# Last cross attention: scores computed a second time in transposed form, sums of weights by columns of ones, no transposes of weights

## The chip, the cores and the metric

The kernel runs on one core of one Trainium2 chip. A core has a matrix engine (TensorE, in the profile PE for its matrix instructions and PEld for the loading of their stationary operand), a vector engine (VectorE, DVE), an activation engine (ScalarE, ACT), a general engine (GpSimd, POOL) and a queue engine (SyncE, SP) that issues transfers. The engines run side by side, each through its own list of instructions in order, and wait for each other by semaphores. The metric is the time of one execution on the device in microseconds (us). Durations inside an execution are read from one profiled execution.

## The reference

Four transformer blocks are applied in turn to `x` (8 sequences of 112 rows, 256 wide). All read one context, `ctx_768` (8 x 375 rows, 192 wide), and everything is fp32. Blocks L0 to L2 have heads of 64; the change touches the last block, L3, with 16 heads of 16. Its middle part is the last cross attention, cut here to what is computed:

```
h = layernorm(x, ln2_w, ln2_b)
q = (h   @ q_w + q_b).reshape(B, T, 16, 16)      # B=8, T=112
k = (enc @ k_w + k_b).reshape(B, S, 16, 16)      # S=375
v = (enc @ v_w + v_b).reshape(B, S, 16, 16)
attn = einsum('bhtd,bhsd->bhts', q, k) * 16**-0.5
attn = where(enc_mask[:, None, None, :], -inf, attn)
attn = softmax(attn, axis=-1)
ca   = einsum('bhts,bhsd->bthd', attn, v)
x    = x + ca.reshape(B, T, 256) @ out_w + out_b
```

Ahead of it stands a masked self attention of the same block (heads of 16, T x T scores), behind it a feed-forward part: `x + gelu(layernorm(x) @ mlp1_w + b) @ mlp2_w + b`, 256 to 1024 to 256.

## The kernel before

**Stages and steps.** The work is numbered in stages: 0 to 2 are block L0 (self attention, cross attention, feed-forward), 3 to 5 block L1, 6 the one attention of L2, 7 the masked self attention of L3, 8 the last cross attention, 9 the last feed-forward. An attention stage is a run of steps. Stage 8 has 32 steps: 8 sequences, and for each four groups g of four heads, the heads 8(g//2) + 2r + g%2 for r = 0..3. The four heads of a step lie on four different groups of 32 rows of the matrix engine. Two heads (of even and odd number) share such a group of 32 rows, 16 rows each; the key tile holds both, and there are two query tiles, one for each parity e, with zeros in the rows of the other parity, so that a product 32 rows deep gives the scores of one head.

**One step of stage 8.** `emit_s` writes the scores of the four heads, 112 queries by 375 keys each, into two PSUM tiles of two banks (four matmuls, L1078). The pool `ps_s` of these tiles has just two, so the next step's scores wait for both to be read. `softmax` (its branch for heads of 16) has VectorE add the mask, negate, and take the minimum, in one custom instruction for each head (L1011), with the result in SBUF; ScalarE takes the exponential of each head and accumulates its sum into a column of `bsums` (L1019). `emit_t` turns the weights, which stand as queries by keys, into keys by queries: for each of three chunks of keys (128, 128, 119) four transposes on TensorE (L1108) into one PSUM bank, and a copy to SBUF by ScalarE (chunks 0 and 2, L1118) or VectorE (chunk 1, L1115). `emit_pv` multiplies with the values (12 matmuls, L1141), which stand 32 columns a head with zeros in 16 of them, so that a pair of steps (both parities) accumulates into one PSUM tile; the second step of the pair copies it to `oT` (L1154).

**Once for each sequence** `emit_norm` takes the reciprocal of the 16 sums of each query (L1182), GpSimd spreads it to 256 columns (`rb`, L1183), and `emit_scale` transposes that in two pieces (L1189) and multiplies `oT` by it (L1198). Then the output product runs for a group of 128 rows of `x` (two chunks, L680) and VectorE adds it to `x` (L684).

**Filling jobs.** Keys of stage 8 come from a key job for each sequence (two products into two PSUM banks, L832 and L841, and two evacuations with the bias, L350 or L358). Values come from value jobs, two chunks of keys at a time (L907, L916), spread over the value tile by `spread_values` (GpSimd zeroes, L811, and VectorE adds the bias, L812). There are such jobs for normalisation, for its transposes, for queries, and for the feed-forward behind.

**What sets the order.** A planner in Python, `Plan`, writes the order of TensorE's work: every piece is an item with a cost in us, a due time, what it uses and makes, and what it has to come after. The main items of a step are S (scores), E (the second half of the exponentials), T (transposes, one item a chunk) and PV. The main loop (from L1610) goes through the steps; in each it emits the scores of a step ahead, the PV of two finished steps together, the T items of the next step with `plan.fill` after each, and then the rest of the filling jobs by the pace of the whole. The steps of stage 7 for late sequences are woven into the first half of stage 8. The other engines take their work in the order that the scheduler gives. Queries, keys and values live in one SBUF ring (`arena`, 10700 columns).

**Loads that the change touches.** `add_last_square` loads the three square weights of L3 into one tile (three transfers, L530); `add_masks` loads both masks to all rows (L560, L561) and multiplies the context mask out to `cm` by eight GpSimd instructions (L590); `bias_columns` (L415) turns small rows into columns of scales and biases.

Of the kernel before, what the change touches and what calls it, by code (L numbers as in the profile page):

```python
# [21 lines left out]
P = 128  # L22
# [9 lines left out]
EPS = 1e-5  # L32

# [271 lines left out]
def kernel(ctx: ExitStack, tc: tile.TileContext, a: dict, out: bass.AP):  # L305
# [3 lines left out]
    ARENA = 10700  # L309
# [16 lines left out]
    plan = Plan(RINGS, ARENA, lambda k: 512 if k[0] == "v" or k[0] == "q" and k[1] in TURNED else S if k[0] == "k" and k[1] in (1, 4, 6, 8) else 4 * T)  # L326
# [3 lines left out]
    def place(key):  # L330

        lo, hi = plan.place[key]
        t = arena[:, lo:hi]
        return t.rearrange("p (i t) -> p i t", i=2) if key[0] == "q" or hi - lo == 4 * T else t
# [7 lines left out]
    def evac(dst, src, n, scale=None, bias=None):  # L342
# [4 lines left out]
        if la <= ld:  # L347
# [58 lines left out]

    brows = const.tile([8, P], F32, name="brows")
    erows = const.tile([1, 2, P], F32, name="erows")
# [3 lines left out]
    bcols = const.tile([P, 10], F32, name="bcols")  # L412
    qcols = const.tile([P, 2, 4], F32, name="qcols")

    def bias_columns():  # L415
        ps = mm_tile()
        nc.tensor.transpose(ps[:, :8], brows, ident[:8, :8])
        for e in range(2):
            nc.tensor.transpose(ps[:, 8 + e : 9 + e], erows[:, e, :], ident[:1, :1])
        nc.vector.tensor_copy(bcols, ps[:, :10])  # L420
        for e in range(2):
            nc.vector.tensor_scalar_mul(qcols[:, e, :], bcols[:, 0:4], bcols[:, 8 + e : 9 + e])

# [8 lines left out]
    ctxB = const.tile([2 * KB, B * S], F32, name="ctxB")  # L432
# [91 lines left out]
    def add_last_square(key, names):  # L524


        def fn():
            t = wpool.tile([P, len(names), 2, D], F32, tag="w", name="squares")
            for i, (k, name) in enumerate(names):
                nc.sync.dma_start(t[:, i, :, :], a[name].rearrange("(c p) n -> p c n", p=P))  # L530
                got[k] = t[:, i, :, :]
# [21 lines left out]
    def add_masks():  # L553
# [4 lines left out]
        def load():  # L558
            m8 = wpool.tile([P, B * (T + S)], U8, tag="w", name="m8")
            nc.sync.dma_start(m8[:, : B * T], a["mask_BxS_bf0"].rearrange("b t -> (b t)").partition_broadcast(P))  # L560
            nc.sync.dma_start(m8[:, B * T :], a["mask_BxS2_bf0"].rearrange("b s -> (b s)").partition_broadcast(P))  # L561
# [20 lines left out]
        def place():  # L582
            got[key] = wpool.tile([T, B, S], BF16, tag="w", name="cm")

        plan.add_load(Item(("load", key), 0, place, makes=[key]))
        for b in range(B):

            def ctx_mask(b=b):
                c = B * T + b * S
                nc.gpsimd.tensor_scalar_mul(got[key][:, b, :], got[src][:T, c : c + S], NEG)  # L590

            plan.add(Item(("mask", b), 0, ctx_mask, first_of(7, 0) - 6 + 0.5 * b, uses=[src, key], seg=SEG[6]))

# [214 lines left out]
    def spread_values(t, ps, rows, bias):  # L808


        nc.gpsimd.memset(t.rearrange("p (g f) -> p g f", f=64)[:rows, :, 16:48], 0.0)  # L811
# [8 lines left out]
    def add_key_jobs(st, b, w, deadline, last=False):  # L820
# [4 lines left out]
        for u in range(1 if last else 4):  # L825
            keys = [("k", st, b, 2 * u + i) for i in range(2)]
            cell = []

            def begin(u=u, cell=cell):
# [8 lines left out]
            def fn(u=u, keys=keys, cell=cell):  # L838
                for i in range(2):
# [4 lines left out]
                    )  # L844
                for i in range(2):
                    t = place(keys[i])
                    evac(t, cell[i][:, :S], S, None, bcols[:, 6 + i : 7 + i] if last else None)
                    got[keys[i]] = t

            plan.add(Item(("kj", st, b, u), 2.1, fn, deadline(b, u), uses=[w], makes=keys, deps=ctx_deps(b),  # L850
                          seg=SEG[st], begin=begin))
# [39 lines left out]
    def add_last_values(st, w, deadline):  # L891
# [4 lines left out]
        for pair in pairs:  # L896
# [3 lines left out]
            def lhs(t, r, b, c):  # L900
                k0, kl = KCH[c]
                return t[r, b * S + k0 : b * S + k0 + kl]

            def begin(pair=pair, cell=cell):
                for b, c in pair:
                    ps = mm_tile()
                    nc.tensor.matmul(  # L907
                        ps[: KCH[c][1], :D], lhsT=lhs(ctxA, slice(0, KA), b, c), rhs=got[wv][:, 0:D],
# [4 lines left out]
            def fn(pair=pair, keys=keys, cell=cell):  # L913
                for n, (b, c) in enumerate(pair):
                    r = slice(n * KB, (n + 1) * KB)
                    nc.tensor.matmul(  # L916
                        cell[n][: KCH[c][1], :D], lhsT=lhs(ctxB, r, b, c), rhs=got[wv][r, D:],
                        start=False, stop=True,
                    )
                for n, (b, c) in enumerate(pair):  # L920
                    t = place(keys[n])
                    spread_values(t, cell[n], KCH[c][1], got[("ctx", "row")])
# [26 lines left out]
    steps = []  # L949
# [289 lines left out]

    def cross_step(st, dh, b, g, turn=False):  # L1240
        at[(st, b, g)] = len(steps)
        j, tb = b // 2, (b % 2) * T
        if dh == 64:
# [446 lines left out]
```

## Time and profile before

| | before |
|---|---|
| time, median of three runs | 1608.58 us (1606.09 to 1613.75) |
| the profiled execution | 1611.6 us, span of its instructions 1609.8 us |
| mean granted clock of TensorE in it | 0.981 |
| TensorE busy | 1534.6 us, 95% of the span |
| weight load busy | 1035.7 us, 64% |
| VectorE busy | 866.6 us, 54% |
| ScalarE busy | 724.5 us, 45% |
| GpSimd busy | 553.9 us, 34% |
| first scores of stage 8 | at 1376.4 us of the span |
| last output product of stage 8 | at 1577.4 us |

Busy time counts an engine's own work, not waiting, and engines overlap. The granted clock is the share of full speed at which TensorE is let run. In a line of instructions the tile written stands before the arrow and those read behind it, with their shapes; `x4` is the number of instructions. A matmul in fp32 shows as two matrix instructions, a transpose as one. In a line of a group the figures are the count, the busy time, the mean of one in ns, and the idle time of the engine just ahead of them with what ended it. `L1078` is line 1078 of the kernel.

### The profile page before, as it was taken

What the parts mean: (1) busy time and instruction counts of PE and PEld (TensorE: products, weight loads), DVE (VectorE), ACT (ScalarE), POOL (GpSimd) and SP (SyncE); (2) the same over time, 40 slices, a digit from 0 to 9 for tenths busy, and PEclk for the clock granted to TensorE, in tenths of its full rate; (3) what the DMA queues carried; (4) which work ended last, traced back from release to release, by engine and by line L of the source; (5) the groups of instructions that cost most, each with busy time, mean ns of one, the idle gap of its engine ahead of it and who ended that gap; (6) DMA issues with size and microseconds to landing.
All of it is one profiled execution on the core that took longest, in us unless ns stands there. A gap on an engine that the chain in (4) does not pass through costs nothing.

```text
span 1609.8 us, 28327 instructions
## 1 busy us (share of the span) xinstructions
PE 1534.6 (95%) x10452; PEld 1035.7 (64%) x10452; DVE 866.6 (54%) x1994; ACT 724.5 (45%) x2364; POOL 553.9 (34%) x801
## 2 busy tenths in 40 slices
PE   9998999999899989999999899899999997999999
PEld 8776666565558877665665566565566555666667
DVE  3664565565422265655656532355566674677662
ACT  3452444444321444444444331244455554687672
POOL 1334343444402234443434321443433346222110
PEclk9999999999999999999999999998999997999999
DMA  5175477667401046457576611045567677200000
GB/s 179 38 210 152 135 218 223 172 191 209 137 30 53 23 134 205 147 176 220 161 202 195 190 50 39 0 115 180 164 193 228 179 222 211 68 2 2 2 1 23
DMA packets 128305, 212.49 MB, mean 132 GB/s; under 512 B 11287, under 2 KB 112295, under 8 KB 128167
## 3 DMA queue, kind: packets, MB, share of 16 engines
q1 hardware_dynamic: 127927, 210.52, 44.6%
q8 instruction: 82, 1.34, 0.3%
q14 instruction: 56, 0.46, 0.1%
q10 hardware_dynamic: 240, 0.17, 0.0%
HBM read 122.45 MB, written 87.43 MB: 130 GB/s over the span
## 4 chain that ended last, share of the span: by engine, by line
PE 78%; DVE 6%; ACT 5%; issue 4%; DMA 4%; POOL 2%; SPq 0%; DVEq 0%; ACTq 0%; POOLq 0%
PE mm L680 12%; PE mm L714 10%; PE mm L1141 10%; PE s L1078 9%; PE mm L866 7%; PE mm L832 7%; PE mm L875 4%; PE mm L841 4%; PE mm L1387 3%; PE mm L791 3%; DMA stage<-b 3%; PE mm L1108 3%; ACT pr L1035 2%; DVE stage L1056 2%; PE mm L1422 2%
## 5 line engine op out<-in xcount | busy, mean ns | idle before, releaser
L1042 POOL TENSOR_TENSOR pr<-pr,rinv 128x750 f32<-128x750 f32 (+3 forms) x224 | 327.4, 1474 | 324.0 <-DVE rinv L1040 323.4
L1035 ACT ACTIVATE pr<-s,nm 128x375 f32<-128x375 f32 (+3 forms) x640 | 302.1, 492 | 252.3 <-DVE nm L1029 204.7
L1078 PE MATMUL s<-arena 64*128 64x375 f32 (+6 forms) x1792 | 223.7, 406 | 18.9 <-ACT pr L1035 13.6
L1056 DVE STREAM_TRANSPOSE stage<-pr 128x768 f32<-128x768 f32 (+2 forms) x218 | 206.5, 969 | 50.3 <-POOL pr L1042 41.3
L1029 DVE TENSOR_REDUCE nm<-s 128x2 f32<-128x750 f32 (+3 forms) x224 | 205.8, 950 | 36.5 <-PE s L1078 35.0
L354 ACT COPY arena<-mm 128x375 f32<-128x375 f32 (+4 forms) x197 | 100.6, 516 | 276.8 <-PE mm L875 125.1
L1141 PE MATMUL mm<-stage,arena 128*64 128x112 f32 (+5 forms) x3840 | 190.1, 269 | 18.0 <-DMA stage<-b 12.6
L1141 PEld LDWEIGHTS mm<-stage,arena 128*64 128x64 f32 (+5 forms) x3840 | 168.9, 134 | 59.5 <-issue 21.3
L1078 PEld LDWEIGHTS s<-arena 64*128 64x128 f32 (+3 forms) x1792 | 122.1, 183 | 108.1 <-issue 33.0
L362 DVE COPY arena<-mm 128x375 f32<-128x375 f32 (+5 forms) x175 | 102.4, 596 | 152.9 <-PE mm L875 82.5
L1019 ACT ACTIVATE pr<-pr,nm 112x375 f32<-112x375 f32 (+2 forms) x256 | 124.5, 491 | 29.5 <-DVE nm L1011 27.9
L1035 ACT ACTIVATION_READ_ACCUMULATOR pr<-s,nm 128x1 f32 (+1 forms) x640 | 135.1, 211 | 0.0
L610 POOL TENSOR_TENSOR rs<-ve,mhalf 128x1 f32<-128x1 f32 x70 | 39.6, 566 | 248.2 <-DVE ve L608 246.4
L1040 DVE RECIPROCAL rinv<-sums 128x2 f32<-128x2 f32 (+3 forms) x224 | 37.8, 169 | 135.8 <-ACT pr L1035 134.7
L866 PE MATMUL mm<-L_xattn_Wv,ctxA 128*128 128x512 f32 (+1 forms) x192 | 93.7, 611 | 2.6 <-ACT arena L352 1.3
L832 PE MATMUL mm<-ctxA,L_xattn_Wk 128*128 128x375 f32 x256 | 93.3, 490 | 2.3 <-ACT hT L350 1.3
L1001 POOL MEMSET pr<- 128x9 f32 (+1 forms) x218 | 22.6, 107 | 210.2 <-DVE stage L1056 192.3
L714 PE MATMUL mm<-hT,L_xattn_Wq 128*128 128x224 f32 x384 | 82.4, 361 | 3.5 <-DVE arena L362 1.5
L684 DVE TENSOR_TENSOR x<-mm,x 128x256 f32<-128x256 f32 x70 | 29.4, 420 | 101.9 <-PE mm L680 101.9
L1108 PEld LDWEIGHTS mm<-ident,pr 112*128 112x128 f32 (+2 forms) x600 | 66.8, 153 | 22.9 <-issue 9.3
L1108 PE MATMUL mm<-ident,pr 112*128 112x112 f32 (+2 forms) x600 | 77.3, 268 | 4.1 <-ACT pr L1019 3.2
L680 PE MATMUL mm<-L_xattn_Wo,oT 128*128 128x256 f32 x336 | 79.1, 390 | 0.8 <-ACT oT L354 0.8
(136 smaller groups left out, 2258.3 us busy)
## 6 DMA issues: line engine op xcount, KB each, us to landing
b<-stage SPq DMA_DIRECT2D x344, 192.0 KB, 3.6
stage<-b SPq DMA_DIRECT2D x86, 768.0 KB, 5.8
b<-stage SPq DMA_DIRECT2D x144, 128.0 KB, 3.8
stage<-b SPq DMA_DIRECT2D x36, 512.0 KB, 4.6
L_xattn_Wo<-in_L_xattn_Wo_dram SPq DMA_DIRECT2D x3, 1024.0 KB, 14.9
L_xattn_w_ff<-in_L_xattn_w_ff_dram SPq DMA_DIRECT2D x3, 1024.0 KB, 8.5
L_xattn_Wv<-in_L_xattn_Wv_dram SPq DMA_DIRECT2D x4, 512.0 KB, 6.8
L_xattn_Wq<-in_L_xattn_Wq_dram SPq DMA_DIRECT2D x2, 1024.0 KB, 6.0
```

Of the source, the lines that this page charges most:

```text
L680: nc.tensor.matmul(ps[:, :D], lhsT=oT[:, c, t * P : (t + 1) * P], rhs=got[wv or w][:, c, :], start=(c == 0), stop=(c == n - 1),)
L714: nc.tensor.matmul(ps[:, i * 2 * T : (i + 1) * 2 * T], lhsT=got[w][:, k, m * P : (m + 1) * P], rhs=hT[:, k, lo:hi], start=(k == 0), stop=( ...
L832: nc.tensor.matmul(ps[:, :S], lhsT=got[wv][:, (2 * u + i) * P : (2 * u + i + 1) * P], rhs=ctxA[:, cols], start=True, stop=False,)
L866: nc.tensor.matmul(ps[: KCH[c][1], :], lhsT=lhs(ctxA, slice(0, KA), c), rhs=got[w][:, hf * 512 : (hf + 1) * 512], start=True, stop=False,)
L1019: return nc.scalar.activation(pr, pr, AF.Exp, bias=nm, scale=-1.0, accum_out=bsums[(st, b)][:, h : h + 1])
L1029: nc.vector.tensor_reduce(nm[:, :, :ns], sv, AX.X, ALU.max, negate=True)
L1035: nc.scalar.activation(pr[:, bk, sl, :], sv[:, bk, sl, :], AF.Exp, bias=nm[:, bk, sl : sl + 1], accum_out=sums[:, bk, sl : sl + 1],)
L1042: nc.gpsimd.tensor_tensor(pr, pr, rinv[:, :, :ns].unsqueeze(3).to_broadcast([rows, 2, ns, nk]), ALU.mult)
L1056: nc.vector.transpose(dst, src)
L1078: nc.tensor.matmul(tiles[i][:, n % 2, (n // 2) * nk : (n // 2 + 1) * nk], lhsT=qap(h), rhs=kap(h), start=True, stop=True,)
L1108: nc.tensor.transpose(pt[:kl, m * T : (m + 1) * T], cell[h][:, c * P : c * P + kl], ident[:T, :T])
L1141: nc.tensor.matmul(po[p0 : p0 + dp, blk * T : (blk + 1) * T], lhsT=got[vk][:kl, hv * dp : (hv + 1) * dp], rhs=wt, start=(c == 0 and par(h) ...
```

## The change

In stage 8 the weights are not transposed any more. The step's scores are computed as before and used for one thing only, their maximum over the keys (two `tensor_reduce` of VectorE over two heads each, negated). The maxima of four heads are columns 16(1-e) + 32r of a tile of zeros; TensorE transposes it, and VectorE adds it (after a minimum that bounds it) into the query tile, into a row that is unused for this parity. The keys are therefore kept twice, one tile for each parity, each with zeros in the other head's rows but for a row of ones, against the maximum, and a row with the mask, against a row of ones in the queries. So a second set of 12 matmuls gives the scores with keys on the rows, masked and less the maximum, into the same two PSUM tiles; two exponentials of ScalarE write the weights (125 rows by 672), and the 12 products with the values read them. Keys are cut 125, 125, 125. A value tile has ones in the 16 columns a head where zeros were; the sums of the weights come out in 16 rows of the result, and for each sequence one matmul with a selecting tile spreads them, VectorE takes the reciprocal of 128 x 448 in PSUM and multiplies. The result then has 512 rows instead of 256, so the output weight is padded with zero rows and the product takes four chunks. The key job makes four evacuations and has four transfers copy the mask row from DRAM; the mask is multiplied out once (8 x 375). The main loop orders these steps so: scores of step n+1, transposed maxima of step n (T 0), the jobs in between, transposed scores of step n (T 1).

```diff
-    ARENA = 10700
+    ARENA = 10550
...
-            t = wpool.tile([P, len(names), 2, D], F32, tag="w", name="squares")
-            for i, (k, name) in enumerate(names):
-                nc.sync.dma_start(t[:, i, :, :], a[name].rearrange("(c p) n -> p c n", p=P))
-                got[k] = t[:, i, :, :]
+            t = wpool.tile([P, 2 * len(names) + 2, D], F32, tag="w", name="squares")
+            for i, (k, name) in enumerate(names[:-1]):
+                got[k] = t[:, 2 * i : 2 * i + 2, :]
+                nc.sync.dma_start(got[k], a[name].rearrange("(c p) n -> p c n", p=P))
+            k, name = names[-1]
+            got[k] = t[:, 2 * len(names) - 2 :, :]
+            nc.gpsimd.memset(got[k], 0.0)
+            w = a[name].rearrange("(m r e d) n -> m r d e n", r=4, e=2, d=16)
+            for m in range(2):
+                for r in range(4):
+                    nc.sync.dma_start(got[k][32 * r : 32 * r + 16, 2 * m : 2 * m + 2, :], w[m, r])
...
-        for b in range(B):
-            def ctx_mask(b=b):
-                c = B * T + b * S
-                nc.gpsimd.tensor_scalar_mul(got[key][:, b, :], got[src][:T, c : c + S], NEG)
+        def ctx_mask():
+            nc.gpsimd.tensor_scalar_mul(got[key], got[src][:B, B * T :], NEG)
+            got["masks"] = bounce.tile([B, S], F32, tag="masks", name="masks")
+            nc.sync.dma_start(got["masks"], got[key])
...
+            def spread(cell=cell, keys=keys):
+                for e in range(2):
+                    t = place(keys[e])
+                    for i in range(2):
+                        evac(t[:, i, :], cell[i][:, :S], S, pcols[:, e : e + 1], kcols[:, e, i : i + 1], i == 0)
+                    at = AUG(e) + 1
+                    rows = t.rearrange("(g f) i k -> f g i k", f=32)[at]
+                    for i in range(2):
+                        nc.sync.dma_start(rows[:, i, :], got["masks"][b : b + 1, :].to_broadcast([4, S]))
...
+        def emit_s():
+            tiles = [ps_s.tile([T, 2, 512], F32, tag="s", name="s") for _ in range(2)]
+            for r in range(4):
+                nc.tensor.matmul(
+                    tiles[r // 2][:, r % 2, :S], lhsT=got[qk][rows(r), m, cols], rhs=got[kk][rows(r), m, :],
+                    start=True, stop=True,
+                )
+            for i in range(2):
+                nc.vector.tensor_reduce(top[:, 2 * i : 2 * i + 2], tiles[i][:, :, :S], AX.X, ALU.max, negate=True)
...
+        def emit_max():
+            pt = mm_tile()
+            nc.tensor.transpose(pt[:, :T], nm, ident[:T, :T])
+            q = got[qk][:, m, cols]
+            nc.vector.scalar_tensor_tensor(q, pt[:, :T], -0.01 * NEG, q, ALU.min, ALU.add)
...
+        def emit_w():
+            tiles = [ps_s.tile([CH, 2, 512], F32, tag="s", name="s") for _ in range(2)]
+            for c in range(3):
+                for r in range(4):
+                    nc.tensor.matmul(
+                        tiles[r // 2][:, r % 2, c * T : (c + 1) * T],
+                        lhsT=got[kk][rows(r), m, c * CH : (c + 1) * CH], rhs=got[qk][rows(r), m, cols],
+                        start=True, stop=True,
+                    )
+            for i in range(2):
+                if e:
+                    w = ppool.tile([CH, 6 * T], F32, tag="pr", name="wt")
+                else:
+                    w = stage[:CH, 768 * (g + i) : 768 * (g + i) + 6 * T]
+                wt.append(w.rearrange("p (r x) -> p r x", r=2))
+                nc.scalar.activation(wt[i], tiles[i][:, :, : 3 * T], AF.Exp)
...
+        def emit_pv():
+            po = pairs.pop((st, b, m)) if e else mm_tile()
+            for c in range(3):
+                for r in range(4):
+                    h = 8 * m + 2 * r + e
+                    nc.tensor.matmul(
+                        po[rows(r), e * T : (e + 1) * T], lhsT=got[("v", st, b, 0, c)][:CH, 32 * h : 32 * h + 32],
+                        rhs=wt[r // 2][:, r % 2, c * T : (c + 1) * T], start=(c == 0), stop=(c == 2),
+                    )
...
+            def emit_scale():
+                dst = oT[:, 0:4, b * T : (b + 1) * T]
+                ps = mm_tile()
+                nc.tensor.matmul(ps[:, : 4 * T], lhsT=sel, rhs=dst, start=True, stop=True)
+                nc.vector.reciprocal(ps[:, : 4 * T], ps[:, : 4 * T])
+                nc.vector.tensor_tensor(dst, dst, ps[:, : 4 * T].rearrange("p (c t) -> p c t", t=T), ALU.mult)
...
-    add_products(8, 9, w("sq"), 2, after_norm(8), norm_by(9), ("sq", "oc"))
+    add_products(8, 9, w("sq"), 4, after_norm(8), norm_by(9), ("sq", "oc"))
...
+            if i + 1 in lasts:
+                plan.main(("T", i + 1, 1))
+                left -= plan.fill(min(left, 0.8))
...
+            if nxt < hi and nxt in lasts and nxt <= i + 3 and clear(nxt):
+                left -= plan.fill(0.4 * left)
+                plan.main(("S", nxt))
+                nxt += 1
...
+            if i + 2 in lasts and plan.items[("S", i + 2)].done:
+                left -= plan.fill(0.5 * left)
+                plan.main(("T", i + 2, 0))
```

## The prediction

> **What bounds the kernel now.** I read the busy table of the page first, then busy time in stretches of 40 us through the last cross attention, then the instructions of TensorE there in order of time, and last the groups of instructions by shape in the last 400 us.
>
> ```profile
> PE 1534.6 (95%) x10452; PEld 1035.7 (64%) x10452; DVE 866.6 (54%) x1994; ACT 724.5 (45%) x2364; POOL 553.9 (34%) x801
> ```
>
> TensorE is busy 95% of the span, so an edit counts by what it does to TensorE's work or to its idle time. In the stretches (columns: length, then busy time of TensorE, weight load, VectorE, ScalarE, GpSimd, then granted clock and DMA) the stage of the change shows the same, at 37.4 to 38.4 us of 40:
>
> ```profile
> 1400.00:1440.00 40.00, 37.36 (x466) 26.57 (x465) 31.54 (x143) 34.10 (x127) 6.20 (x15) 1.00 0.01 2
> 1440.00:1480.00 40.00, 38.39 (x434) 26.68 (x437) 30.19 (x105) 30.00 (x87) 9.99 (x17) 1.00 0.01 2
> 1480.00:1520.00 40.00, 37.36 (x401) 26.27 (x397) 28.25 (x117) 29.75 (x101) 9.20 (x14) 0.91 0.01 2
> ```
>
> From 1400 to 1560 TensorE idles 7 us, with 2.7 more from 1382: about 10. VectorE and ScalarE have a quarter free, and relieving them alone gives nothing. The order of TensorE's work (start, length, line, operands, matrix instructions; a matmul is two, a transpose one):
>
> ```profile
> 1421.39 1.46 PE L832 MATMUL mm<-ctxA,ctx_w 128*128 128x375 f32 x4
> 1422.78 0.90 PE L841 MATMUL mm<-ctxB,ctx_w 64*128 64x375 f32 x4
> 1423.61 0.66 PE L1078 MATMUL s<-arena 32*112 32x112 f32 x16
> 1424.20 1.40 PE L1108 MATMUL mm<-ident,pr 112*128 112x112 f32 x12
> 1425.53 1.12 PE L1078 MATMUL s<-arena 32*112 32x112 f32 x16
> 1426.58 1.36 PE L1141 MATMUL mm<-stage,arena 128*32 128x112 f32 x48
> 1427.87 1.11 PE L1108 MATMUL mm<-ident,pr 112*112 112x112 f32 x8
> 1428.82 1.04 PE L907 MATMUL mm<-ctx_w,ctxA 128*128 128x256 f32 x4
> 1429.79 0.70 PE L916 MATMUL mm<-ctx_w,ctxB 64*128 64x256 f32 x4
> 1430.42 0.90 PE L1078 MATMUL s<-arena 32*112 32x375 f32 x8
> 1431.25 0.41 PE L1189 MATMUL mm<-ident,rb 112*128 112x112 f32 x2
> ```
>
> Start to start this prices: 12 weight transposes 1.33, a key job 2.22 (L832, L841), 8 narrow score matmuls .59, the weighted sums of two steps 1.29 (L1141), a value job 1.60 (L907, L916), the scores of a step .83, the two transposes of the sums .25. A score tile is handed on and used at once, since between scores and sums lie other steps' transposes. The groups by shape, last 400 us (count, then busy, mean ns, idle before):
>
> ```profile
> L1019 ACT ACTIVATE pr<-pr,nm 112x375 f32<-112x375 f32 x128 | 76.7, 604 | 21.5 <-DVE nm L1011 21.3
> L1011 DVE CUSTOM_DVE_ANT_0 pr<-s,cm 112x375 f32<-112x375 f32 x128 | 62.6, 544 | 4.3 <-PE s L1078 3.9
> L1108 PE MATMUL mm<-ident,pr 112*128 112x112 f32 x256 | 35.4, 269 | 3.5 <-ACT pr L1019 3.2
> L1029 DVE TENSOR_REDUCE nm<-s 128x2 f32<-128x750 f32 x28 | 25.0, 930 | 1.6 <-PE s L1078 1.4
> L1182 DVE RECIPROCAL rsum<-bsums 112x16 f32<-112x16 f32 x11 | 2.7, 249 | 5.9 <-ACT pr L1019 5.9
> ```
>
> **TensorE's work.** Gone: 32 sets of 12 transposes by 1.28 (they stand 1.24 to 1.33 apart) = 41.0, and eight pairs of sum transposes by .25 = 2.0. Added: 32 sets of 12 transposed score matmuls, 32 rows deep and 112 wide, which the 8 narrow scores price at .59 x 12/8 = .88, so 28.2 (from below the 12 sums matmuls of a step, .65, so 20.8); 32 transposes of the maxima by .13 = 4.2; eight column-sum matmuls 448 wide by .5 (estimate from the 375-wide key matmuls of L841, .42 each) = 4.0; output products of four chunks in place of two, seven token groups by .97 (1.13 as listed, .97 to the next start) = 6.8. Together 43.2 for 43.0, **+0.2 us**, between -7 (by the bound from below) and +13 (a set at the 1.28 of the twelve transposes it replaces); the narrow scores are the nearest row, the same operation with the same depth.
>
> **The new chain.** Scores and transposed scores share the same two PSUM tiles, and each uses both. So from the end of one set of transposed scores to the end of the next: first exponential .85 (125x672; the gate activation of the feed-forward, 128x384 in .58 and 128x512 in .69, has a slope of .86 ns a column), scores .75, the two maxima 2 x .93, the addition into q .30, the handovers .2, the transposed scores .9: **4.85 us a step** of which TensorE works 1.65. The rest has two gaps: .97 before the scores (the exponential holds the tile) and 2.17 before the transposed scores (VectorE's maxima and addition). A gap is idle unless TensorE has other work queued in exactly that place. Its order in the changed kernel says what stands there, priced with the rows above:
> - Second gap: in ten steps nothing but the maxima's transpose (.13) or that and a sums pair: 20 us idle. Two with little work: 2.6. Seven with a value job: .44 each, 3.1. The steps with a key job (2.22) are closed. Sum 26.
> - First gap: scores follow at once or after a .25 job in six places, after .5 to .86 in four: 6.
> - Column sums: VectorE takes the reciprocal of 128x448. Rows of 2, 8 and 16 columns last 163, 197 and 249 ns, 6.1 ns a column, so 2.9 us for 448; at the copy's slope (448 in .62) it would be .6. I take 2.9, the row of the same operation. It and the multiply (.39) stand between maxima in VectorE's order, and in six of eight places hold the next maxima and so the chain: 6 x 3.0 = 18.
> Idle 50 against 10 before: **+40 us** (bounds: 12 with a cheap reciprocal and half of the second gap filled, 55 with VectorE's other work, such as value spreads at .41, queued in front of maxima).
>
> The Trainium skill, "VectorE: DVE Perf Modes", section "First, the fixed hardware budget", says that Reciprocal iterates its divide with a repeat count of 8; at its 0.96 GHz I estimate 3.7 us for 448 columns, which would make the 18 us about 23. No row here shows a wide reciprocal.
>
> **Start of the stage.** The first key job stands at 1352.7 now, before an idle of 4.43 us that ends at 1359.89. In the changed order it comes behind that idle, directly before the first scores: +2.2; and these wait for four evacuations and four mask-row transfers (a copy in SBUF lands in 2.1 us, an attention write in 3.6), of which other products hide most: +1.3, bounds 0 and 5. **+3.5.**
>
> **Clock.** After a mere 1.16 us of idle the scores took 2.53 us instead of .90, and the stretch 1490 to 1500 ran at a granted clock of .66, which lost some 3.4 us:
>
> ```profile
> 1491.27 2.53 PE L1078 MATMUL s<-arena 32*112 32x375 f32 x8 [1.16 <-DVE nm L1011]
> 1493.73 1.72 PE L1141 MATMUL mm<-stage,arena 112*32 112x112 f32 x32
> 1495.38 2.56 PE L1108 MATMUL mm<-ident,pr 112*128 112x112 f32 x12
> ```
>
> With five times the idle I add two such spells: **+7** (bounds: 0, if most gaps pass, as those before this one did; 50, if the clock is .75 through the stage's 168 us of work, 168/.75 = 224 less 6).
>
> The Trainium skill, "TensorE: Matmul & The Clock Gate", Part 1, halves the clock after an idle window of about 3.4 us; no single gap above is that long, so by it the 7 would be 0. Its Part 4 says that transposes do not count as activity; by that the change, which takes 384 of them out, would even keep the clock up. The row above, cold after 1.16 us, makes me keep the 7.
>
> **Costed at nothing.** ScalarE loses 128 exponentials with their accumulations and the copies, and gains 64 of .83; VectorE swaps 128 x .54 for 64 x .93: neither set the pace. Sixteen more key evacuations (.6) fill their slack; if it is gone, those in front of a maximum add to the 55 above. SyncE issues 32 mask-row transfers in the stage, at .35 to .45 each 11 to 14 us; its last load is at 1377.1, nothing is queued behind. Earlier the output weight goes in eight small transfers instead of one, behind a GpSimd memset: 3.2 us more of issue near 1231. The attention sends behind it, eight spread over 8.7 us from 1232.4, have about 6 us of slack; without it, up to 3. GpSimd loses seven mask operations of 1.16 us near 1341 to 1351 for which nobody waited, and the value fills only get wider.
>
> **Sum.** 1611.6 (the profiled execution; span 1609.8) + 0.2 + 40 + 3.5 + 7 = 1662.3. The median of the three runs is 3.0 below the profiled one: **1659 us**.
>
> **Rivals.**
> 1. Gaps filled (faster): the scheduler's woven jobs cover both gaps, and the transposed scores run at the price of the sums. Then 1611.6 - 7.2 (work) - 7 (idle of before) - 3.4 (its cold spell) - 3 = 1591. It decides when the idle of the stage stays under some 3 us, which needs score tiles of their own for the second scores, or maxima of well under half of .93. For it: VectorE and ScalarE lose a third of their load. Against: ten steps with nothing queued.
> 2. Milder: reciprocal at .6 (-11.5) and no cold spell (-7), perhaps some gap shorter: 1625 to 1645.
> 3. Clock lost through the stage: TensorE never gets a long busy stretch: +50 less the 7, and part of it lies in gaps: 1678 to 1720. For it the row at 1491; against, the clock of 1.00 in the neighbouring stretches.
> 4. No change: part of 1, with the idle of before kept: about 1605 to 1612.
>
> **How the numbers follow.** Half a percent, 8 us, is what a measurement here tells from no change. Chances: forecast (1645 to 1678) .52, milder .20, clock .13, gaps filled .09, no change .06. So faster .09, same .06, slower .85. The low end 1620 leaves out rivals 1 and 4; the high end 1698 leaves out the worse part of rival 3; together about .2.
>
> **What the profile will show.** If right: TensorE idle before the transposed scores, released by VectorE's maxima or addition, and before scores, released by the exponential; about 50 us of idle in a stage some 50 us longer; a 128x448 reciprocal near 2.9 us; VectorE and ScalarE busy time down all the same; 384 fewer transposes. Wrong if the waits are a few tenths, if the reciprocal is short, if the clock stays at 1.00, or if transposed scores cost far from .88 a set.

## The result and the profile after

The changed kernel took 1706.08 us (median of four runs, 1702.39 to 1709.38) against 1608.98 us for the kernel before (four runs, 1606.09 to 1613.75): a ratio of 1.059, 95% interval 1.0572 to 1.0608. It is slower by 97 us, where 50 were forecast. The profiled execution after took 1707.91 us, its span 1706.1 us, its mean granted clock .955.

The busy table of the page of the kernel after:

```profile
PE 1585.0 (93%) x10900; PEld 1057.6 (62%) x10900; DVE 882.4 (52%) x1807; ACT 667.5 (39%) x2124; POOL 543.6 (32%) x794
```

ScalarE lost 57 us of work, as the change meant it to. TensorE's busy time nevertheless grew by 50 us, and its idle time by 46 (75 to 121). The next two answers give the busy time in the stage, from the first scores of L3's last self attention steps ahead of it to the last output product behind it. The columns are the stretch, its length, busy time of TensorE, weight load, VectorE, ScalarE, GpSimd, and then granted clock, DMA share and GB/s. First before:

```profile
1347.70:1577.44 229.74, 213.04 (x2203) 148.25 (x2203) 153.71 (x594) 161.69 (x502) 50.25 (x85) 0.96 0.11 34
```

Then after:

```profile
1358.03:1676.36 318.33, 261.59 (x2659) 168.63 (x2659) 166.16 (x401) 107.67 (x265) 44.52 (x77) 0.85 0.08 23
```

The stage is 88.6 us longer: 40.0 more idle (16.7 to 56.7) and 48.6 more busy. The granted clock fell from .96 to .85. Length times the part of the clock that is missing (in what follows the missing clock; a clock of two decimals makes it good to 1.5 us) is 9.2 us before and 47.7 after, 38.5 more. By the records of the clock in the trace some of that falls on idle time, where it costs nothing: TensorE works for 15.2 us at half clock before and for 83.6 after, so at most 34 of the 48.6 us are the clock's. The rest of the 97 us lies ahead of the stage, which began 10.3 us later, less 2.6 us in the tail, where some feed-forward work had moved into the stage.

The groups of instructions of the stage after, by shape (count, then busy, mean ns, idle before and its releaser), show which waits they are:

```profile
L1314 DVE TENSOR_REDUCE nmx<-s 112x2 f32<-112x750 f32 x64 | 57.4, 932 | 31.2 <-PE s L1309 31.0
L1309 PE MATMUL s<-arena 32*112 32x375 f32 x256 | 41.7, 579 | 8.8 <-ACT wt L1339 4.5 <-DMA arena<-masks 2.7 <-DVE nm L1064 1.4
L1328 PE MATMUL s<-arena 32*125 32x112 f32 x768 | 36.6, 331 | 24.0 <-DVE arena L1321 24.0
L711 PE MATMUL mm<-squares,oT 128*128 128x256 f32 x77 | 26.2, 488 | 8.8 <-DVE oT L1372 8.8
L1371 DVE RECIPROCAL mm<-mm 128x448 f32<-128x448 f32 x8 | 23.7, 2964 | 6.1 <-PE mm L1370 6.1
```

TensorE waits 24.0 us ahead of the transposed scores (L1328; L1309 are the first scores, L1314 their maxima), for the addition into the query tile that comes behind the maxima; 8.8 us ahead of the scores (L1309), half of it for the exponential that still reads the shared tile; and 8.8 us ahead of output products (L711), for the multiplication behind the reciprocal, which takes 2.96 us. Those are the forecast gaps. What they do to the clock shows in TensorE's order of time after:

```profile
1398.89 0.38 PE L1242 MATMUL mm<-ident,rb 128*128 128x128 f32 x2
1400.64 0.92 PE L1328 MATMUL s<-arena 32*125 32x112 f32 x24 [1.37 <-DVE arena L1321]
1401.49 3.31 PE L786 MATMUL mm<-hT,L_xattn_qkv_w 128*128 128x224 f32 x8
1404.73 0.99 PE L1309 MATMUL s<-arena 32*112 32x375 f32 x8
1405.66 0.32 PE L1319 MATMUL mm<-ident,nmx 112*128 112x112 f32 x1
1408.84 1.62 PE L1328 MATMUL s<-arena 32*125 32x112 f32 x24 [2.87 <-DVE arena L1321]
1410.39 3.35 PE L786 MATMUL mm<-hT,L_xattn_qkv_w 128*128 128x224 f32 x8
1413.67 1.35 PE L1347 MATMUL mm<-stage,arena 125*32 125x112 f32 x24
```

After an idle of 1.37 us the query product of eight instructions takes 3.31 us, where the same product took 1.78 before; after one of 2.87 us the transposed scores take 1.62 instead of .92 and the next query product 3.35. The stretches of 1.5 us there (same columns as above; the clock is the third from the end):

```profile
1401.00:1402.50 1.50, 1.50 (x26) 1.32 (x20) 0.00 (x0) 0.82 (x2) 0.00 (x0) 0.69 0.00 0
1402.50:1404.00 1.50, 1.50 (x6) 1.36 (x5) 0.00 (x0) 0.53 (x1) 0.00 (x0) 0.50 0.00 0
1404.00:1405.50 1.50, 1.50 (x11) 0.57 (x9) 0.39 (x1) 0.16 (x1) 0.00 (x0) 0.67 0.00 0
1405.50:1407.00 1.50, 0.47 (x5) 0.14 (x1) 1.18 (x3) 0.73 (x2) 0.00 (x0) 1.00 0.00 0
1407.00:1408.50 1.50, 0.00 (x0) 0.00 (x0) 1.50 (x4) 0.78 (x2) 0.00 (x0) 0.96 0.00 0
1408.50:1410.00 1.50, 1.16 (x20) 1.16 (x24) 0.28 (x2) 0.00 (x0) 0.00 (x0) 0.50 0.00 0
1410.00:1411.50 1.50, 1.50 (x15) 1.23 (x8) 0.00 (x0) 1.01 (x2) 0.00 (x0) 0.50 0.04 11
1411.50:1413.00 1.50, 1.50 (x6) 1.35 (x5) 0.00 (x0) 0.34 (x1) 0.00 (x0) 0.50 0.00 0
```

The clock is full during nearly all of the idle and one half afterwards. By its records it is lowered from 1401.57 to 1404.98 and from 1408.39 to 1415.22, for 3.4 and 6.8 us, nearly all of it spent on full work. All changes of the clock in this stage lie a whole multiple of 3.41 us apart, so the clock goes by stretches of that length and not by single gaps. Of the stretches at full clock, none of the 40 in which TensorE idled less than .9 us was followed by a lowered one; of 14 with .9 to 1.6 us of idle six were, and with more than that all ten. In all the stage has 16 lowered spells, 3.4 to 10.2 us long, where it had two before, and 20 gaps of 1 us or more, where it had five.

### The profile page after: what moved, and what is told of

Same layout as the page of the kernel before. It is cut to its first block, busy times and chain, and to the rows that moved or that the text cites. A ratio compares the mean times of both kernels' runs of the same rounds, so it can differ in the third digit from the quotient of the medians.

```text
span 1706.1 us, 28869 instructions
## 1 busy us (share of the span) xinstructions
PE 1585.0 (93%) x10900; PEld 1057.6 (62%) x10900; DVE 882.4 (52%) x1807; ACT 667.5 (39%) x2124; POOL 543.6 (32%) x794
## 4 chain that ended last, share of the span: by engine, by line
PE 78%; DVE 8%; DMA 4%; ACT 4%; issue 3%; POOL 2%; SPq 1%; DVEq 0%; ACTq 0%; POOLq 0%
PE mm L711 12%; PE mm L745 9%; PE mm L1194 8%; PE s L1131 8%; PE mm L920 7%; PE mm L883 6%; PE mm L1518 6%; PE mm L929 4%; PE mm L892 4%; PE mm L822 3%; DMA stage<-b 3%; ACT pr L1088 2%; PE s L1328 2%; DVE stage L1109 2%; PE mm L1347 2%
## 5 line engine op out<-in xcount | busy, mean ns | idle before, releaser
L1131 PE MATMUL s<-arena 64*128 64x375 f32 (+5 forms) x1536 | 195.7, 389 | 23.0 <-ACT pr L1088 14.5
L1194 PE MATMUL mm<-stage,arena 128*64 128x112 f32 (+3 forms) x3072 | 169.0, 271 | 24.2 <-DMA stage<-b 21.6
L1194 PEld LDWEIGHTS mm<-stage,arena 128*64 128x64 f32 (+3 forms) x3072 | 151.8, 141 | 56.3 <-issue 14.6
L1131 PEld LDWEIGHTS s<-arena 64*128 64x128 f32 (+3 forms) x1536 | 114.0, 187 | 104.0 <-ACT pr L1088 27.8
L711 PE MATMUL mm<-L_xattn_Wo,oT 128*128 128x256 f32 x336 | 80.3, 395 | 0.8 <-ACT oT L359 0.8
L652 POOL TENSOR_SCALAR xn<-x,mv,rs 128x256 f32<-128x256 f32 x63 | 77.1, 1224 | 6.4
L745 PEld LDWEIGHTS mm<-hT,L_xattn_Wq 128*128 128x128 f32 x384 | 70.2, 190 | 12.3 <-issue 4.6
L711 PEld LDWEIGHTS mm<-L_xattn_Wo,oT 128*128 128x128 f32 x336 | 64.6, 197 | 16.7 <-issue 4.7
```

What stands on the lines that cost most here:

```text
L711: nc.tensor.matmul(ps[:, :D], lhsT=oT[:, c, t * P : (t + 1) * P], rhs=got[wv or w][:, c, :], start=(c == 0), stop=(c == n - 1),)
L745: nc.tensor.matmul(ps[:, i * 2 * T : (i + 1) * 2 * T], lhsT=got[w][:, k, m * P : (m + 1) * P], rhs=hT[:, k, lo:hi], start=(k == 0), stop=( ...
L1131: nc.tensor.matmul(tiles[i][:, n % 2, (n // 2) * nk : (n // 2 + 1) * nk], lhsT=qap(h), rhs=kap(h), start=True, stop=True,)
L1194: nc.tensor.matmul(po[p0 : p0 + dp, blk * T : (blk + 1) * T], lhsT=got[vk][:kl, hv * dp : (hv + 1) * dp], rhs=wt, start=(c == 0 and par(h) ...
```

## The experiments

Two theories stood after the result. **Theory A**: the forecast gaps are there, and they cost a second time, because TensorE's clock is lowered behind it. **Theory B**: the added matrix work is dearer than priced, and the low clock goes along with it. This table has for each kernel with the changed stage one profiled execution: when the stage begins, its length, TensorE's busy and idle time in it, the granted clock, the missing clock, what follows the stage, and beside them the ratio of the time to the kernel before's.

| kernel | begins | length | busy | idle | clock | missing | tail | ratio (interval) |
|---|---|---|---|---|---|---|---|---|
| before | 1347.7 | 229.7 | 213.0 | 16.7 | .96 | 9.2 | 32.4 | 1 |
| after | 1358.0 | 318.3 | 261.6 | 56.7 | .85 | 47.7 | 29.7 | 1.059 (1.0572 to 1.0608) |
| matmuls in gaps | 1358.5 | 300.7 | 256.9 | 43.9 | .92 | 24.1 | 29.8 | 1.0473 (1.0446 to 1.0500) |
| transposes in gaps | 1353.0 | 300.5 | 254.6 | 46.0 | .92 | 24.0 | 29.8 | 1.0463 (1.0431 to 1.0496) |
| copy for reciprocal | 1354.8 | 299.4 | 255.2 | 44.3 | .86 | 41.9 | 29.7 | 1.0458 (1.0435 to 1.0482) |
| maxima transposed first | 1357.1 | 303.1 | 256.5 | 46.6 | .89 | 33.3 | 29.7 | 1.0498 (1.0463 to 1.0533) |
| maxima of a third | 1359.0 | 279.7 | 233.4 | 46.3 | .88 | 33.6 | 29.8 | 1.0359 (1.0337 to 1.0380) |
| shorter reciprocal | 1350.8 | 312.7 | 266.8 | 45.9 | .85 | 46.9 | 26.2 | 1.0503 (1.0483 to 1.0522) |
| three edits | 1349.9 | 264.1 | 237.2 | 26.9 | .90 | 26.4 | 26.2 | 1.0178 (1.0155 to 1.0201) |

### Work in the gaps, in two kinds

```diff
             nc.tensor.transpose(pt[:, :T], nm, ident[:T, :T])
+            if 4 * b + g in (1, 2, 5, 6, 10, 12, 14, 20, 22, 26, 28, 29):
+                junk = mm_tile()
+                for _ in range(3):
+                    nc.tensor.matmul(junk[:, :D], lhsT=ident, rhs=ctxA[:, :D], start=True, stop=True)
```

> The changed kernel with 36 matmuls more that nobody reads: in twelve steps whose second gap (between scores and transposed scores) holds hardly any other work, three matmuls 128x256 by 128x128 into a spare PSUM bank, some 1.4 us each time. Theory A (the lost clock): TensorE's busy time grew by 46 us from the first key job of the stage to its last product because the gaps throw the granted clock to one half; kept busy, it keeps its clock, and the time falls by 15 to 35 us although 17 us of work are added. Theory B (dearer work): the added matmuls simply cost more than I priced and the clock in the records is a by-product; the extra work fills idle time and the time stays within 4 us, or grows.

It took 1688.10 us; by the ratios 19 us less than the changed kernel, with 36 matmuls more. The groups by shape of its stage:

```profile
L1332 PE MATMUL s<-arena 32*125 32x112 f32 x768 | 30.9, 292 | 11.0 <-DVE arena L1325 10.9
L1323 PE MATMUL mm<-ctxA,ident 128*128 128x256 f32 x72 | 19.0, 403 | 0.0
```

The idle ahead of the transposed scores fell from 24.0 to 11.0 us, which by itself changes nothing, since work took its place. But the same 768 score instructions now took 30.9 us instead of 36.6, and although 19.0 us of busy time were added the total of the stage fell by 4.7. The clock went from .85 to .92, its missing part from 47.7 to 24.1 us. This is theory A; theory B allowed no gain.

The second kind had ten transposes in each of the same twelve gaps:

```diff
-                for _ in range(3):
-                    nc.tensor.matmul(junk[:, :D], lhsT=ident, rhs=ctxA[:, :D], start=True, stop=True)
+                for n in range(10):
+                    nc.tensor.transpose(junk[:, P * (n % 4) : P * (n % 4) + P], ident, ident)
```

> The changed kernel with the same twelve gaps filled as in the run with 36 added matmuls, which cost 18 us less than the changed kernel, but with ten transposes of 128x128 (about 1.3 us) in place of three matmuls each. The Trainium skill (TensorE: Matmul & The Clock Gate, Part 4) says that transposes do not count as activity. By that the granted clock of the stage stays at .85 and the time within 4 us of the changed kernel. If transposes count like matmuls, the clock rises to about .92 and the time falls by 12 to 20 us; then the 384 transposes that the change removed had themselves been keeping the clock up.

It took 1684.77 us, by the ratios 20 us less than the changed kernel, with the clock at .92. Its stage by the same columns as above:

```profile
1352.99:1653.50 300.51, 254.55 (x2779) 168.35 (x2779) 166.01 (x401) 107.61 (x265) 44.50 (x77) 0.92 0.09 27
```

So transposes kept the clock up here just as matmuls did. What Part 4 of the page named there states of transposes does not hold for this case, and the removed 384 were no mere burden: while they ran, TensorE was not idle. That they alone kept the gaps closed before is not shown.

### The reciprocal, in four forms

A copy in its place leaves the weights unnormalised and prices the whole of it:

```diff
-                nc.vector.reciprocal(ps[:, : 4 * T], ps[:, : 4 * T])
+                nc.vector.tensor_copy(ps[:, : 4 * T], ps[:, : 4 * T])
```

> The changed kernel with the reciprocal of 128x448 replaced by a copy in place, so the weights stay unnormalised and are multiplied by their sum; only the time is of use. The forecast has eight reciprocals of 2.9 us, six of them holding the chain, 18 us; a copy takes .6. If so, 12 us less idle, and with the clock that goes with it (theory A) 15 to 30 us less time. Rival: what waits for the reciprocal has slack, the products can come late, and the maxima have spare time: 0 to 5 us less.

It took 1684.91 us, by the ratios 21 us less. The idle fell by 12.5 us, as the forecast's step says, but not where it says. The groups of the stage with the copy:

```profile
L1328 PE MATMUL s<-arena 32*125 32x112 f32 x768 | 35.8, 325 | 21.6 <-DVE arena L1321 21.6
L711 PE MATMUL mm<-squares,oT 128*128 128x256 f32 x76 | 21.2, 420 | 0.0
L1371 DVE COPY mm<-mm 128x448 f32<-128x448 f32 x8 | 5.0, 631 | 6.8 <-PE mm L1370 6.8
```

The wait of the output products went from 8.8 us to nothing, that of the transposed scores from 24.0 to 21.6 only. The reciprocal cost its time mostly by holding the products behind it in TensorE's order, and less by holding the maxima.

Next, the same result with the reciprocal on GpSimd:

```diff
-                nc.vector.reciprocal(ps[:, : 4 * T], ps[:, : 4 * T])
-                nc.vector.tensor_tensor(dst, dst, ps[:, : 4 * T].rearrange("p (c t) -> p c t", t=T), ALU.mult)
+                inv = ppool.tile([P, 4 * T], F32, tag="pr", name="inv")
+                nc.scalar.copy(inv, ps[:, : 4 * T])
+                nc.gpsimd.tensor_tensor(inv, inv, mone.to_broadcast([P, 4 * T]), ALU.pow)
+                nc.gpsimd.tensor_tensor(dst, dst, inv.rearrange("p (c t) -> p c t", t=T), ALU.mult)
```

> The changed kernel with the reciprocal taken off VectorE: ScalarE copies the spread sums to SBUF, GpSimd raises them to -1 and multiplies. The result is the same; only the engine changes. If the reciprocal cost its time by holding VectorE, and with it the maxima and the chain, most of the 21 us that the copy in its place saved come back: 12 to 22 us less than the changed kernel. If it was the output product waiting for the end of the reciprocal (2.1 to 2.5 us idle ahead of it, four times), GpSimd, which takes at least as long, gains nothing: within 5 us, or slower.

It took 2259.79 us. GpSimd's costliest group, whole run:

```profile
L1375 POOL TENSOR_TENSOR inv<-inv,mone 128x448 f32<-128x448 f32 x8 | 574.1, 71766 | 110.0 <-ACT inv L1374 91.5 <-DMA arena<-masks 18.5
```

One power of 128x448 takes 71.8 us, 160 ns a column. The run answers nothing about VectorE; it priced an operation that I had seen only on one column (.57 us). The same edit stood in a run together with two others, for which it says as little:

> Three edits at once: maxima over 125 keys only (37 us less by itself), the transposed maxima ahead of the next scores (15 less), the reciprocal on GpSimd. If they act on the same waits, the sum stays far below 52: 40 to 50 less than the changed kernel, 1655 to 1665. If each takes its own part of the chain and the clock recovers as the idle shrinks, more than their sum: 60 to 85 less, 1620 to 1645. It beats the kernel before (about 1610) only if the 8 to 10 us that are lost ahead of the stage are regained too, which none of the edits touches.

It took 2227.37 us, again set by the eight powers.

Last, a shorter reciprocal without loss: the sums are gathered on 128 rows by 112 queries first, and spread after it. For room its ring has 10080 columns.

```diff
-                nc.tensor.matmul(ps[:, : 4 * T], lhsT=sel, rhs=dst, start=True, stop=True)
-                nc.vector.reciprocal(ps[:, : 4 * T], ps[:, : 4 * T])
+                for c in range(4):
+                    nc.tensor.matmul(ps[32 * c : 32 * c + 32, :T], lhsT=pick,
+                                     rhs=oT[:, c, b * T : (b + 1) * T], start=True, stop=True)
+                nc.vector.reciprocal(inv, ps[:, :T])
...
+                for c in range(4):
+                    nc.tensor.matmul(ps[:, c * T : (c + 1) * T], lhsT=sel[:, c, :], rhs=inv, start=True, stop=True)
```

> The changed kernel with a shorter reciprocal and nothing left out: a small matmul for each of the four chunks gathers the sums of the sixteen heads on 128 rows by 112 queries, VectorE takes the reciprocal of that (128x112, .84 us by the slope of 6.1 ns a column), and four matmuls spread it before the multiplication. If the wide reciprocal of 2.96 us cost its time as an occupant of VectorE ahead of maxima and products, some 2.1 us are saved eight times and the clock with it: 15 to 20 us less than the changed kernel, close to the 21 us of the copy in its place. If the extra matmuls and the second job for each sequence cost as much: within 6 us.

It took 1691.56 us, by the ratios 14 us less, just under the range. The reciprocal took .85 us instead of 2.96, and the idle of the stage fell by 10.8 us, nearly as with the copy and in the same places: the wait of the output products is gone, that of the transposed scores is 21.2 us; the additional matmuls and the unchanged clock gave 5 us of busy time back. Stage and tail together gained 9 us. The other 7 lie ahead of the stage, where this kernel differs by its ring and its selecting tiles only; which of them, if any, did it was not separated.

### The chain through the score tiles

The transpose of the maxima ahead of the next scores:

```diff
+            if i + 2 in lasts and plan.items[("S", i + 2)].done:
+                plan.main(("T", i + 2, 0))
             if nxt < hi and nxt in lasts and nxt <= i + 3 and clear(nxt):
                 left -= plan.fill(0.4 * left)
                 plan.main(("S", nxt))
                 nxt += 1
...
-            if i + 2 in lasts and plan.items[("S", i + 2)].done:
-                left -= plan.fill(0.5 * left)
-                plan.main(("T", i + 2, 0))
```

> The changed kernel with the transpose of the maxima of step n put ahead of the scores of step n+1 on TensorE instead of behind them, so that transpose and addition can run in the first gap. If the chain through the shared tiles is what makes the second gap, it loses the .15 of the transpose, the .27 of the addition and two handovers, .5 us, in some twenty steps: 10 us of idle, with the clock 10 to 25 us of time. Rival: VectorE, whose order the scheduler sets, still adds behind the maxima of the next step, and nothing is gained (within 5 us).

It took 1691.63 us, by the ratios 15 us less. The idle fell by 10.2 us, as much as .5 us in twenty steps, 8.5 of it ahead of the transposed scores; the missing clock fell by 14.

The first scores and maxima over a third of the keys:

```diff
-                    tiles[r // 2][:, r % 2, :S], lhsT=got[qk][rows(r), m, cols], rhs=got[kk][rows(r), m, :],
+                    tiles[r // 2][:, r % 2, :CH], lhsT=got[qk][rows(r), m, cols], rhs=got[kk][rows(r), m, :CH],
...
-                nc.vector.tensor_reduce(top[:, 2 * i : 2 * i + 2], tiles[i][:, :, :S], AX.X, ALU.max, negate=True)
+                nc.vector.tensor_reduce(top[:, 2 * i : 2 * i + 2], tiles[i][:, :, :CH], AX.X, ALU.max, negate=True)
```

> The changed kernel with the first scores and the maxima taken over the first 125 keys only: what is subtracted is the maximum of a third of the keys, which cancels in the weights. TensorE's work falls by about 32 x .55 = 18 us, the two maxima from .93 to about .33 each, and so the chain by 1.75 us a step. If the chain makes the idle, 25 to 30 of the 56 us of idle in the stage go, and with them most of the lost clock (theory A): 60 to 85 us less in all. With theory B, and idle that comes from elsewhere (the products, the reciprocal): only the 18 us of work and some 10 of idle, 20 to 35 us less.

It took 1668.90 us, by the ratios 37 us less: 2 us above the range of theory B and far below that of A, so by itself this run does not speak for A. Of the idle just 10.4 us went instead of 25 to 30. The wait ahead of the transposed scores fell from 24.0 to 10.4 us, but that ahead of the scores grew from 8.8 to 11.6. Of the 46.3 us that were left, 11.3 lay at the start of the stage, 9.2 ahead of the products (the reciprocal) and 5.6 ahead of scores for the exponential (the chain through the tiles has a second half that this edit does not touch). Two examples from the start and one of each of the others, in TensorE's order of time of this kernel:

```profile
1371.84 2.51 PE L1194 MATMUL mm<-stage,arena 128*64 128x112 f32 x24 [7.80 <-DMA stage<-b]
1386.36 0.78 PE L1309 MATMUL s<-arena 32*112 32x125 f32 x8 [2.89 <-DMA arena<-masks]
1486.49 0.47 PE L1309 MATMUL s<-arena 32*112 32x125 f32 x4 [0.88 <-ACT wt L1339]
1560.90 3.78 PE L711 MATMUL mm<-squares,oT 128*128 128x256 f32 x8 [2.39 <-DVE oT L1372]
```

Then the three edits at once (maxima of a third, transposed first, shorter reciprocal):

> That shorter reciprocal together with the maxima over 125 keys and the transposed maxima ahead of the next scores. By themselves they took 15 to 20 (expected), 37 and 15 us. If they act on separate links of one chain and the clock comes back as the idle shrinks: 1625 to 1645. If the idle that is left is that of the exponentials on the shared score tiles, which none of them touches (.88 us ahead of scores, in most steps), they overlap: 1645 to 1660.

It took 1639.85 us. Stage and tail are 58 us shorter than after; the three by themselves gave 39, 15 and 9. They add up almost fully (58 of 63), so they cut separate links. The idle of 26.9 us is 10 above that of the kernel before, and yet the clock stands at .90 and not .96: it has eight lowered spells, the first of 13.7 us at the start of the stage, where the kernel before has two. It is the fastest form that was run, and 1.8% slower than the kernel before: no form here beats it.

### What lies ahead of the stage

The changed kernel and its variants enter the stage late, at 1350 to 1359 us instead of 1347.7. Two edits of the kernel before looked for the cause. The shorter ring alone:

```diff
-    ARENA = 10700
+    ARENA = 10550
```

> The kernel before with nothing changed but the length of the SBUF ring for queries, keys and values, 10550 columns instead of 10700. The changed kernel and its variants come to the first self attention scores of L3's late sequences 7 to 11 us later than the kernel before (1354.8 to 1359.0 against 1347.7 of the span). If the shorter ring is the cause (tiles placed and freed in another way), this kernel is 5 to 8 us slower than the kernel before; if the cause lies in the new columns, small tiles and loads, or in nothing that repeats, it stays within 3 us.

It took 1612.82 us beside 1611.16 (ratio 1.0008, interval .9994 to 1.0022): nothing. And all preparations of the changed kernel, with the ring:

```diff
+    erows = ctxB[:1, B * S - 6 * P :].rearrange("p (e f) -> p e f", f=P)
...
+    sel = const.tile([P, P], F32, name="sel")
...
+    maxima = [const.tile([T, P], F32, name=f"nmx{e}") for e in range(2)]
...
-        for e in range(2):
+        for e in range(6):
             nc.tensor.transpose(ps[:, 8 + e : 9 + e], erows[:, e, :], ident[:1, :1])
```

> The kernel before with the preparations of the changed one alone: the longer start (more rows turned to columns, a selecting tile, two zeroed tiles, the context tile placed earlier) and the shorter ring. Up to the loads of the square weights the order of all engines is then that of the changed kernel. The changed kernel and its variants are 5 to 8 us late by 1200 us of the span, half of it gained between 416 and 740 us, where no instruction differs. If the preparations cause it, this kernel is 5 to 8 us slower than the kernel before; if it stays within 3 us, the delay must come from what stands later.

It took 1615.24 us beside 1610.57 (ratio 1.0033, interval 1.0018 to 1.0048), entering the stage at 1352.5. So the preparations cost some 5 us, without any instruction of the attention being different. How they do it (where tiles lie, which moment a transfer meets) is not shown. What the changed kernel and its variants are late beyond that stays open: the starts of kernels with equal code up to there differ by up to 6 us between profiles (1353.0 to 1359.0).

## Why the prediction was wrong

The direction was right, the size not: 97 us where 50 were forecast, and one term made most of the difference.

- **TensorE's work (+0.2):** right, at full clock. Start to start the transposed scores take .85 a set (predicted .88), the maxima's transpose .15 (.13), the column sums .75 to .86 (.5), the products of four chunks 1.84 for eight instructions, .87 more each time (.97). With these 44.7 us are added for 43.0 removed.
- **Gaps (+40):** right in size. The stage's idle grew by 40.0 us; 4.8 of that lie at its start (7.68, .49 and 2.73 us of waits instead of 4.43, 1.08 and .63), so the gaps gave 35. The second gap's 24.0 us answer to the 26 forecast, those ahead of the scores, without the 2.7 for the masks, to the 6. The reciprocal's 18 were 12.5 by the copy, through products that wait and hardly through maxima: the term was a third too large and its path was wrong.
- **Reciprocal:** 2.96 us, forecast 2.9 from the slope of three rows; the 3.7 that was estimated from the Trainium skill ("VectorE: DVE Perf Modes", section "First, the fixed hardware budget") was too long.
- **Start (+3.5):** 4.8 as idle.
- **Busy times:** ScalarE's fell, but VectorE's, which was to fall too, rose from 866.6 to 882.4 us; the eight reciprocals alone take 23.7.
- **Clock (+7): the step that failed.** It was sized as two further cold spells, "with five times the idle", while its own bound from above was 50 us. There were 14 more (16 for two), and the missing clock grew by 38.5 us, of which at most 34 cost time. The price of one was about right: 3.0 us on the mean, 3.4 in the row at 1491. Their number was wrong. From 1382 to 1560 the kernel before has three gaps of 1 us or more. Two of them passed at a full clock, though they were longer than the 1.16 us that the forecast goes by:

```profile
1390.48 0.32 PE L1108 MATMUL mm<-ident,pr 112*128 112x112 f32 x1 [1.78 <-ACT pr L1019]
1434.67 0.69 PE L907 MATMUL mm<-ctx_w,ctxA 128*119 128x256 f32 x2 [1.80 <-ACT stage L1118]
```

So "most gaps pass" was rightly read. But the forecast itself listed sixteen gaps of 2 us or more (ten steps, six reciprocals); at one in three, five of them would have been cold, about 17 us. That gaps as close as these would be followed by a lowered clock far more often, no row of before could show. Rival 3 named this outcome, at a chance of .13, and the runs with work in the gaps confirm its mechanism: 13 us less idle took 24 us of missing clock away. One more reading was wrong: "no single gap above is that long" leaves out the 4.43 us at the start of the stage; there the clock was at one half from 1359.1 to 1369.3.
- **Ahead of the stage (costed at nothing, up to 3):** 10.3 us late in the profiled executions, of which some 5 are shown to come from the preparations, which had no term at all.
- **Not accounted for:** busy time grew by 48.6 us; at most 34 for the clock, 1.7 for the work and 2.6 for feed-forward work that moved into the stage leave at least 10 us. The ends of instructions ahead of a gap count in full where they are otherwise overlapped; that this is all of it was argued only.
- **Rivals:** rival 1 (gaps filled) fell as argued: ten steps had nothing queued in the gap. No gain from the relief of ScalarE (57 us less busy) is seen. In rival 2 the 11.5 should be 13.8 by the forecast's own figures (six times 2.3, which is 2.9 less .6); nothing hangs on it.

## What to carry to other kernels

Where TensorE is busy 95% of the span, a change that leaves its work equal but opens short gaps in it pays for the gaps twice: here 40 us of idle came with up to 34 us lost to a lowered clock. The second price does not follow from the idle alone: edits that took 10 to 13 us of idle away took 1 us of missing clock (shorter reciprocal), 6 (copy), 14 (both edits of the chain) or 24 (work in the gaps). Nor does one gap tell what many will do: in the kernel before one of three was followed by a lowered clock, with 20 gaps close together there were 16 lowered spells. So a forecast that opens many gaps should carry the clock as a wide term, up to one spell for each gap, until a run shows less. Before removing work from the critical engine, look which buffer the next work will wait for: with the transposes gone, TensorE waits for the hand-over of two score tiles.

## What was not expected of the hardware

- The clock fell to .50 behind idles of 1.37 and 2.87 us, for 3.4 and 6.8 us, and stood at 1.00 during nearly all of the idle itself. The Trainium skill, "TensorE: Matmul & The Clock Gate", Part 1, has the lowering after an idle window of about 3.4 us. The clock's changes here do lie multiples of 3.41 us apart, but an idle of 1.16 us could suffice, while ones of 1.78 and 1.80 passed.
- Transposes kept the clock up as well as matmuls (.92 with either in the same gaps, .85 without), against Part 4 of the same page.
- A power on GpSimd costs 160 ns a column (128x448 in 71.8 us), where one column took .57 us; the reciprocal of VectorE costs 6.6 ns a column (2.96 us), .85 us for 112.
